# Routed experts between attention steps: the first product for 512 tokens at once instead of twice 256

## The chip, the cores and the metric

The kernel runs on one core of one Trainium2 chip. The metric is the device time of one execution in microseconds (us). PE is the matrix engine, PEld its weight loads, DVE the vector engine, ACT the scalar engine, POOL and SP the two engines that here mostly issue DMAs.

## The reference, cut to what matters

Two transformer layers run over 8 sequences of 512 tokens of 256 values, all in 32-bit floats. Layer 0 is a state-space block with a routed feed-forward part of 8 experts. Layer 1, which the change touches, adds two things to its input `x`: a 16-head attention and a top-2 routed feed-forward part with 7 experts and one "no-op" expert. Each expert takes at most 512 tokens (its capacity).

```python
# layer 1, attention: heads of 16 values, 512 x 512 scores for each of 8 sequences
scores = einsum('bhqd,bhkd->bhqk', qh, kh) * scale
scores = clip(clip(scores) * decay)          # a band that falls with |i - j|
out    = einsum('bhqk,bhkd->bhqd', softmax(scores), vh) @ Wo
# layer 1, experts: cap = 512 rows of 256 values for each of 7 experts, I = 1024
h   = relu(einsum('ceh,ehi->cei', inputs, experts_inter))     # first product
out = einsum('cei,eih->ceh', h, experts_out) * in_w[..., None]  # second product
combined = zeros.at[used_idx].add(out) + x_flat * (noop_w * noop_mask)[:, None]
```

## The kernel before, in words

The program writes the order of each engine's instructions by hand; an engine takes its own in that order and waits where data or a buffer is missing. Layer 0 fills the first two thirds of the span. Then comes the attention of layer 1, in 128 **steps** (the loop `for n in range(N + 2)`), one for each sequence `b`, group `g` of four heads, and block `c` of 128 keys. I count steps by `n`, from 0. In a step PE does two things for the attention:

- `scores` (L1554): four matmuls `s_ps` (L1561), each 16 rows of weights against 512 columns, into four PSUM banks of their own tag (`bufs=4`, so there is one set of banks). The four heads lie in four different row strips of the array and run side by side. DVE reads each bank once (L1564: times the band, maximum per row), which frees it. ACT then takes the exponent (L1578).
- `values` (L1584) of the step before the last: four matmuls `o_ps` (L1586), in four different column strips.

Between them PE is given other work by `fill()` (L1729). It has four places in a step: one after the scores, three after the values. Each call puts one **unit** there, from the first of these that has one: a piece already begun (`half_done`), an `urgent` piece (the output projection of a finished sequence, `finish`, L1517, matmuls `fin` at L1521), or the next unit of `experts()` (L1383), and this only while `spent < due()`. `spent` counts the expert units given so far, and `due()` (L1713) grows by the same amount each step, so that all `WORK` units are due at step `LAST` = 117. `WORK` is 238 before. The experts become ready at step 5, so `due()` grows by 238/110 = 2.16 units a step; the first unit goes out in step 8.

Before, an expert is worked in two halves of 256 rows. For each half the units are:

- **T**: four PE transposes (L1399) of the gathered rows into one bank, and a copy on ACT (L1400).
- **H**, eight of them: one block of 128 of the 1024 inner values. Two fp32 matmuls of 128 x 256 (L1407), which the profile shows as four instructions, and one ReLU on ACT (L1410).
- **Y**, eight of them: two fp32 matmuls of 128 x 256 (L1420), again four instructions. Four Y make the 256 outputs of 128 tokens; `yield True` after the first three marks the piece as begun, so the rest follow at the next places whatever `due()` says. After the fourth, ACT scales the result (L1426) and POOL adds it to `x1` in HBM by an indirect DMA (L1427).

I write **F** for a unit of `fin` (four such pieces in a row per sequence). T, H, Y and F share two PSUM banks of one tag (`bank`, L1363). The rows are gathered by indirect DMAs on POOL (`expert_rows`, L1367), two for each half, into two buffers; the two weight matrices of an expert, 1 MB each, come by SP's queue into one buffer each (`expert_w1`, L1378, and L1390).

A step's pattern is written as "after the scores | after the values": "H|H" has one unit in each place, "Y|YYY" one and three, "|" none. The order of PE's instructions can be read from the built program, so these patterns are known for both kernels.

Of the kernel before, what the change touches and what calls it, by code (L numbers as in the profile page):

```python
# [9 lines left out]
FP = mybir.dt.float32  # L10
I32 = mybir.dt.int32
AF = mybir.ActivationFunctionType
# [5 lines left out]
P = 128  # L18
B, S, DM = 8, 512, 256
NT = B * S  # L20
NTILE = NT // P
TPB = S // P
KC = DM // P
# [10 lines left out]
FC = FF // P  # L34
NBLK = (NT + NE * (P - 1)) // P
OFTEN = NBLK - 3
CAP = NT // NE
NE1 = NE - 1
NSLOT1 = NE1 * CAP
HALF = CAP // 2  # L40
# [23 lines left out]
def tile_kernel(ctx: ExitStack, tc: tile.TileContext, t, out: bass.AP):  # L64
    nc = tc.nc
    V, A, G, T, Y = nc.vector, nc.scalar, nc.gpsimd, nc.tensor, nc.sync
# [4 lines left out]
    def ctile(name, shape, dtype=FP, pool=None):  # L71
        return (pool or const).tile(shape, dtype, name=name, tag=name)
# [7 lines left out]
    ident = ctile("ident", [P, P])  # L80
# [38 lines left out]
    xn1 = dram.tile([NT + P, DM], FP, name="xn1", tag="xn1")  # L119
# [115 lines left out]
    def numbers(pool, table, to):  # L235

        none = pool.tile([P, table.shape[1]], FP, name="nu_n", tag="nu_n")
        V.tensor_scalar(none, table[:, :, 0], 0.0, nowhere, ALU.is_equal, ALU.mult)
        V.scalar_tensor_tensor(to, table[:, :, 0], -1.0, none, ALU.add, ALU.add)
# [134 lines left out]
    def bank(name, shape, tag="gen"):  # L374
        return mp.tile(shape, FP, name=name, tag=("e", "s")[tag] if isinstance(tag, int) else tag, bufs=2)
# [194 lines left out]
    with ExitStack() as es:  # L570
# [646 lines left out]
        e2 = None  # L1217
# [141 lines left out]
    with tc.tile_pool(name="a1", bufs=1) as p1, tc.tile_pool(name="a2", bufs=2) as p2, tc.tile_pool(  # L1359
        name="ap", bufs=1, space=PSUM  # L1360
# [3 lines left out]
            return psum.tile(shape, FP, name=name, tag="bank", bufs=2)  # L1364

        late_bank = bank
        def expert_rows(e, half):  # L1367
            xd = e2.tile([P, 2, DM], FP, name="e_xd", tag="e_rows")
            for c in range(2):
                at = e * TPB + half * 2 + c  # L1370
                G.indirect_dma_start(
                    out=xd[:, c, :], out_offset=None, in_=xn1,
                    in_offset=bass.IndirectOffsetOnAxis(ap=number1[:, at : at + 1], axis=0),
                    bounds_check=NT + P - 1, oob_is_err=True,
                )
            return xd

        def expert_w1(e):  # L1378
            w1 = e1.tile([P, KC, FF], FP, name="e_w1", tag="e_w1")
            Y.dma_start(out=w1, in_=t["ei"][e])  # L1380
            return w1

        def experts():  # L1383
            nonlocal number1
            number1 = e1.tile([P, NSLOT1 // P], I32, name="number1", tag="number1")
            numbers(e1, slots, number1)
            w1 = expert_w1(0)
            yield
            xd = expert_rows(0, 0)
            yield  # L1390
            for e in range(NE1):
                w2 = e1.tile([P, FC, DM], FP, name="e_w2", tag="e_w2")
                Y.dma_start(out=w2, in_=t["eo"][e])
                for half in range(2):
                    xdT = e1.tile([P, KC, HALF], FP, name="e_xdT", tag="e_xdT")
                    tp = bank("e_tp", [P, KC, HALF])
                    for k in range(KC):
                        for c in range(2):
                            T.transpose(tp[:, k, c * P : (c + 1) * P], xd[:, c, k * P : (k + 1) * P], ident)  # L1399
                    A.copy(xdT, tp)  # L1400

                    yield
                    hT = e1.tile([P, FC, HALF], FP, name="e_hT", tag="e_hT")
                    for f in range(FC):
                        hp = bank("e_hp", [P, HALF])
                        for k in range(KC):
                            T.matmul(  # L1407
                                hp, w1[:, k, f * P : (f + 1) * P], xdT[:, k, :], start=(k == 0), stop=(k == KC - 1)
                            )
                        A.activation(hT[:, f, :], hp, AF.Relu)  # L1410
                        yield
                    if half == 0:
                        xd = expert_rows(e, 1)
                    elif e + 1 < NE1:
                        w1, xd = expert_w1(e + 1), expert_rows(e + 1, 0)
                    yo = e2.tile([P, 2, DM], FP, name="e_yo", tag="e_yo")
                    for c in range(2):
                        yp = bank("e_yp", [P, DM])
                        for f in range(FC):
                            T.matmul(  # L1420
                                yp, hT[:, f, c * P : (c + 1) * P], w2[:, f, :], start=(f == 0), stop=(f == FC - 1)
                            )
                            if f % 2 == 1 and f < FC - 1:
                                yield True
                        at = e * TPB + half * 2 + c
                        A.mul(yo[:, c, :], yp, slots[:, at, 1:2])  # L1426
                        G.indirect_dma_start(  # L1427
                            out=x1, out_offset=bass.IndirectOffsetOnAxis(ap=number1[:, at : at + 1], axis=0),
                            in_=yo[:, c, :], in_offset=None, bounds_check=NT - 1, oob_is_err=False,
                            compute_op=ALU.add,  # L1430
                        )
                        yield
# [96 lines left out]
        def combine():  # L1529


            def add(b):
                G.dma_start(out=x_sb[:, b * TPB : (b + 1) * TPB, :], in_=rows_of(x1, b), accum_op=ALU.add)

            for b in (B - 1, *range(B - 2)):
                add(b)
            yield
            while B - 2 not in finished:
                yield
            add(B - 2)  # L1540
            for b in range(B - 1):
                G.dma_start(out=rows_of(out, b), in_=x_sb[:, b * TPB : (b + 1) * TPB, :])
# [149 lines left out]
        with tc.manual_schedule(engines=ENGINES):  # L1692
# [13 lines left out]
                G.memset(one, 0.0)  # L1706
            finished = set()
            urgent, idle, chains = [], [], []
            WORK = NE1 * 2 * (1 + FC + 2 * FC // 2)
            LAST = 117  # L1710
            spent = 0

            def due():  # L1713

                return WORK * (n - ready - 2) / (LAST - ready - 2)

            rows, work, ready, e1, number1 = combine(), None, None, None, None
# [28 lines left out]
            def more():  # L1746
                if spent == WORK:
                    next(rows, None)

            def follow():  # L1750

                nonlocal work, ready, e1, e2
                if late_left:
                    pass
                elif ready is None:
                    ready = n
                    tls.close()
                    e1 = es.enter_context(tc.tile_pool(name="f1", bufs=1, side="right"))
                    e2 = es.enter_context(tc.tile_pool(name="f2", bufs=2, side="right"))
                    work = experts()  # L1760
                    next(work)
                elif n == ready + 1:
                    next(work)
# [7 lines left out]
            for n in range(N + 2):  # L1771

                if n < N:
                    b, g, c = steps[n]
# [127 lines left out]
def build(arrays):  # L1902
    import concourse.bacc as bacc

    nc = bacc.Bacc("TRN2", target_bir_lowering=False, num_devices=1)
    t = {
        k: nc.dram_tensor(f"in_{k}_dram", v.shape, mybir.dt.from_np(v.dtype), kind="ExternalInput").ap()
        for k, v in arrays.items()
    }
    out = nc.dram_tensor("out_0_dram", (NT, DM), FP, kind="ExternalOutput").ap()  # L1910
    with tile.TileContext(nc) as tc:
        tile_kernel(tc, t, out)
    return nc
# [10 lines left out]
```

## Time and profile before

| | us |
|---|---|
| median of 3 runs (lowest, highest) | 1805.91 (1796.79, 1808.62) |
| the profiled execution, its own time | 1802.12 |
| its span, first to last instruction | 1800.4 |
| up to step 0 (layer 0) | 1137.2 |
| steps 0 to 7 | 70.5 |
| steps 8 to 118, with the expert units | 533.1 |
| step 119 to the end | 59.6 |

Over the span PE is busy 1630.7 us (91%), DVE 1201.4 (67%), ACT 914.8 (51%), POOL 574.7 (32%). The profile's page has the busy time of each engine, the span in 40 slices with the granted PE clock, the chain of work that ended last, and groups of equal instructions: first the busy time of the group, then the mean of one instruction in ns, then how long its engine had been idle before it and what ended that. A matmul counts as busy from its start to a modelled end, also while PE holds the next one back for a wait, so a PE that reads 100% can still stand. The chain and the timeline give start and length in us, then what ran, and how often.

### The profile page before, as it was taken

The page shows a single profiled execution, that of the slowest core. Times are in us where ns is not written, and L with a number is a line of the kernel's source. Part 1 is how long each engine was busy: PE and PEld are TensorE (multiplying, and loading weights), DVE is VectorE, ACT ScalarE, POOL GpSimd, SP SyncE. Part 2 cuts the span into 40 slices and gives each one's busy share as a digit, 9 for nine tenths or more (in the row PEclk, how much of TensorE's full clock was granted, in tenths as well). Part 3 has the DMA queues.
Part 4 walks back from the last instruction along what each step waited for, and adds up shares of the span by engine and source line. Part 5 has one row for each costly group of instructions (what it writes and reads, how often), then busy time and mean ns, then how long its engine had stood idle before and what let it go on. Part 6 is the DMA issues. An engine that isn't in the chain of part 4 may idle for free.

```text
span 1800.4 us, 25907 instructions
## 1 busy us (share of the span) xinstructions
PE 1630.7 (91%) x8736; PEld 980.5 (54%) x8736; DVE 1201.4 (67%) x3166; ACT 914.8 (51%) x2173; POOL 574.7 (32%) x520
## 2 busy tenths in 40 slices
PE   6556889989999999998798889879999999999997
PEld 6224567667677776775455556444544545444442
DVE  6578586575765765757877575566667666666674
ACT  4232344454454544544544523337767676766674
POOL 0041465475574654754323220001112111211030
PEclk8777799999999999999898898759999999999996
DMA  8010544554475445642644433232433324334163
GB/s 298 6 53 7 168 158 172 188 176 156 155 234 182 159 176 177 208 146 86 145 147 131 124 85 111 91 114 63 126 92 105 116 60 128 87 110 125 48 102 112
DMA packets 131789, 230.56 MB, mean 128 GB/s; under 512 B 20093, under 2 KB 93823, under 8 KB 120512
## 3 DMA queue, kind: packets, MB, share of 16 engines
q1 hardware_dynamic: 101952, 119.46, 21.4%
q0 software_dynamic: 28656, 108.69, 19.8%
q8 instruction: 73, 1.20, 0.3%
q10 hardware_dynamic: 1040, 0.66, 0.1%
q14 instruction: 68, 0.56, 0.1%
HBM read 176.23 MB, written 53.05 MB: 127 GB/s over the span
## 4 chain that ended last, share of the span: by engine, by line
PE 44%; DVE 6%; ACT 1%; issue 1%; DMA 0%; SPq 0%; POOL 0%; DVEq 0%; ACTq 0%
PE s_ps L1561 10%; PE o_ps L1586 8%; PE e_hp L1407 7%; PE e_yp L1420 6%; PE fin L1521 2%; PE qp L265 2%; PE pj L939 2%; PE tab L230 1%; PE pp L765 1%; DVE s L1564 1%; PE op L1084 1%; PE seg L1127 1%; PE yd L1165 1%; PE lp L250 1%; PE e_tp L1399 1%
## 5 line engine op out<-in xcount | busy, mean ns | idle before, releaser
L1564 DVE CUSTOM_DVE_ANT_0 s<-s_ps,band 128x512 f32<-128x512 f32 x512 | 322.9, 687 | 183.0 <-PE s_ps L1561 179.9
L1578 ACT ACTIVATE s<-s,ng 128x512 f32<-128x512 f32 x512 | 335.6, 711 | 0.0
L939 PE MATMUL pj<-xT,w_w_in 128*128 128x512 f32 x384 | 198.5, 643 | 11.7 <-DVE cv L952 7.5
L1561 PE MATMUL s_ps<-qT,kT 16*128 16x512 f32 x1024 | 198.7, 694 | 4.5 <-DMA kT<-kd 4.5
L1427 POOL DMA_INDIRECT x<-e_yo,number x28 | 44.7, 1597 | 445.7 <-ACT w L1574 291.0
L952 DVE SCALAR_TENSOR_TENSOR cv<-pj,w_conv_w,cv 128x511 f32<-128x511 f32 (+2 forms) x192 | 143.1, 746 | 20.5 <-ACT cv L948 16.0
L1111 POOL TENSOR_TENSOR au<-da,half 128x512 f32<-128x512 f32 x64 | 77.6, 1213 | 245.1 <-PE seg L1127 174.2
L1586 PE MATMUL o_ps<-s,wv 128*32 128x512 f32 x1024 | 154.5, 677 | 0.9 <-ACT w L1574 0.9
L642 PEld LDWEIGHTS h_ps<-xdT,w 128*128 128x128 f32 x1152 | 138.9, 194 | 21.3 <-issue 20.5
L642 PE MATMUL h_ps<-xdT,w 128*128 128x128 f32 x1152 | 142.1, 277 | 2.6 <-DMA w<-in_w_dram,w_idx 2.6
L666 PE MATMUL y_ps<-w,hT 128*128 128x256 f32 x576 | 137.9, 383 | 0.0
L1407 PEld LDWEIGHTS e_hp<-e_xdT,e_w 128*128 128x128 f32 x448 | 77.9, 191 | 87.3 <-issue 39.3
L666 PEld LDWEIGHTS y_ps<-w,hT 128*128 128x128 f32 x576 | 108.1, 193 | 29.8 <-issue 16.1
L1407 PE MATMUL e_hp<-e_xdT,e_w 128*128 128x256 f32 x448 | 124.2, 405 | 0.0
L939 PEld LDWEIGHTS pj<-xT,w_w_in 128*128 128x128 f32 x384 | 70.2, 201 | 92.8 <-issue 80.6
L1561 PEld LDWEIGHTS s_ps<-qT,kT 16*128 16x128 f32 x1024 | 66.5, 196 | 86.2 <-DVE peaks L1564 42.9
L1420 PE MATMUL e_yp<-e_w,e_hT 128*128 128x256 f32 x448 | 112.6, 394 | 0.0
L1420 PEld LDWEIGHTS e_yp<-e_w,e_hT 128*128 128x128 f32 x448 | 81.0, 191 | 54.1 <-issue 37.6
L1140 ACT ACTIVATE mt<-seg,mid 64x64 f32<-64x64 f32 x512 | 109.7, 309 | 0.8
L1174 DVE TENSOR_TENSOR yT<-yT,yd 128x512 f32<-128x512 f32 (+1 forms) x64 | 43.7, 683 | 98.0 <-PE yd L1165 97.0
L956 ACT ACTIVATE th<-cv 128x512 f32<-128x512 f32 x64 | 40.3, 630 | 120.1 <-DVE cv L952 107.4
L1159 DVE TENSOR_TENSOR mt<-mt,cbm 128x1024 f32<-128x1024 f32 x64 | 96.5, 1508 | 0.1
(340 smaller groups left out, 2819.8 us busy)
## 6 DMA issues: line engine op xcount, KB each, us to landing
ex<-exd SPq DMA_DIRECT2D x96, 128.0 KB
fr<-fdd SPq DMA_DIRECT2D x64, 128.0 KB
od<-os SPq DMA_DIRECT2D x28, 256.0 KB
e_w<-in_ei_dram SPq DMA_DIRECT2D x7, 1024.0 KB
e_w<-in_eo_dram SPq DMA_DIRECT2D x7, 1024.0 KB
vd<-vt SPq DMA_DIRECT2D x16, 272.0 KB
vt<-vd SPq DMA_DIRECT2D x8, 544.0 KB
u<-in_u_dram SPq DMA_DIRECT2D x8, 512.0 KB
```

The costliest lines, as they stand in the source:

```text
L642: T.matmul(hp[:, i, :], w1[:, k * FF + f * P : k * FF + (f + 1) * P], xdT[:, k * P : (k + 1) * P], start=(k == 0), stop=(k == KC - 1),)
L666: T.matmul(yp, hT[f // 4][:, f % 4, :], w2[:, f * DM : (f + 1) * DM], start=(f == 0), stop=(f == FC - 1),)
L939: T.matmul(pj, w_in[:, k, o * P : (o + 1) * P], self.xT[:, k, :], start=(k == 0), stop=(k == KC - 1))
L952: V.scalar_tensor_tensor(cv[:, s:], pj[:, : S - s], conv_w[:, q, 3 - s : 4 - s], cv[:, s:], ALU.mult, ALU.add)
L1140: A.activation(mt[lo, over, h], seg[lo, over, h], AF.Exp, bias=mid[lo, self.i, h : h + 1])
L1159: V.tensor_tensor(self.mt, self.mt, bc(self.cbm, 1, H3), ALU.mult)
L1407: T.matmul(hp, w1[:, k, f * P : (f + 1) * P], xdT[:, k, :], start=(k == 0), stop=(k == KC - 1))
L1420: T.matmul(yp, hT[:, f, c * P : (c + 1) * P], w2[:, f, :], start=(f == 0), stop=(f == FC - 1))
L1561: T.matmul(sp[i], self.k[r, cols], self.q[r, :], start=True, stop=True)
L1564: V.tensor_tensor_reduce(out=self.p[i], in0=sp[i], in1=band[:, at : at + S], scale=1.0, scalar=KEEP, op0=ALU.mult, op1=ALU.max, accum_out= ...
L1578: A.activation(self.p[i], self.p[i], AF.Exp, bias=self.ng[:, i : i + 1])
L1586: T.matmul(op[32 * i : 32 * i + 32, :], self.wv[:, i, :], self.p[i], start=(self.c == 0), stop=(self.c == TPB - 1),)
```

## The change

The first product is made for all 512 rows of an expert at once. The gathers of both halves are issued together (four instead of two). The transposes go by the two blocks of 128 input values: T is still four transposes into a bank of 128 x 512 and one copy, two T to an expert. H becomes two matmuls of 128 x 512 and one ReLU of 512 columns; eight H to an expert instead of sixteen. The second product keeps its shape and its sixteen Y. The next expert's first weights and gathers are asked for after the last H of an expert, ahead of its sixteen Y. `WORK` becomes 7 x (2 + 8 + 16) = 182; `LAST` and `due()` stay as they are.

```diff
-        def expert_rows(e, half):
-            xd = e2.tile([P, 2, DM], FP, name="e_xd", tag="e_rows")
-            for c in range(2):
...
+        def expert_rows(e):
+            halves = []
+            for half in range(2):
+                xd = e2.tile([P, 2, DM], FP, name="e_xd", tag="e_rows")
+                for c in range(2):
+                    at = e * TPB + half * 2 + c
+                    G.indirect_dma_start(
+                        out=xd[:, c, :], out_offset=None, in_=xn1,
...
+                halves.append(xd)
+            return halves
...
-            xd = expert_rows(0, 0)
+            halves = expert_rows(0)
             yield
             for e in range(NE1):
                 w2 = e1.tile([P, FC, DM], FP, name="e_w2", tag="e_w2")
                 Y.dma_start(out=w2, in_=t["eo"][e])
+                xdT = e1.tile([P, KC, CAP], FP, name="e_xdT", tag="e_xdT")
+                for k in range(KC):
+                    tp = bank("e_tp", [P, CAP])
+                    for c in range(TPB):
+                        T.transpose(
+                            tp[:, c * P : (c + 1) * P], halves[c // 2][:, c % 2, k * P : (k + 1) * P], ident
+                        )
+                    A.copy(xdT[:, k, :], tp)
+                    yield
+                hT = e1.tile([P, FC, CAP], FP, name="e_hT", tag="e_hT")
+                for f in range(FC):
+                    hp = bank("e_hp", [P, CAP])
+                    for k in range(KC):
+                        T.matmul(hp, w1[:, k, f * P : (f + 1) * P], xdT[:, k, :], start=(k == 0), stop=(k == KC - 1))
+                    A.activation(hT[:, f, :], hp, AF.Relu)
+                    yield
+                if e + 1 < NE1:
+                    w1, halves = expert_w1(e + 1), expert_rows(e + 1)
                 for half in range(2):
-                    xdT = e1.tile([P, KC, HALF], FP, name="e_xdT", tag="e_xdT")
-                    tp = bank("e_tp", [P, KC, HALF])
...
-                        hp = bank("e_hp", [P, HALF])
...
-                    if half == 0:
-                        xd = expert_rows(e, 1)
-                    elif e + 1 < NE1:
-                        w1, xd = expert_w1(e + 1), expert_rows(e + 1, 0)
                     yo = e2.tile([P, 2, DM], FP, name="e_yo", tag="e_yo")
                     for c in range(2):
+                        at = half * 2 + c
                         yp = bank("e_yp", [P, DM])
                         for f in range(FC):
                             T.matmul(
-                                yp, hT[:, f, c * P : (c + 1) * P], w2[:, f, :], start=(f == 0), stop=(f == FC - 1)
+                                yp, hT[:, f, at * P : (at + 1) * P], w2[:, f, :], start=(f == 0), stop=(f == FC - 1)
                             )
...
-            WORK = NE1 * 2 * (1 + FC + 2 * FC // 2)
+            WORK = NE1 * (KC + FC + 4 * FC // 2)
```

More of the change, by code (lines that the diff above doesn't have):

```diff
@@ L1366, in tile_kernel @@
         late_bank = bank
-        def expert_rows(e, half):
-            xd = e2.tile([P, 2, DM], FP, name="e_xd", tag="e_rows")
-            for c in range(2):
[L1370 to L1376, printed above, removed]
+        def expert_rows(e):
[6 more added lines that the diff above has]
+                        out=xd[:, c, :], out_offset=None, in_=xn1,
+                        in_offset=bass.IndirectOffsetOnAxis(ap=number1[:, at : at + 1], axis=0),
+                        bounds_check=NT + P - 1, oob_is_err=True,
+                    )
+                halves.append(xd)
+            return halves
         def expert_w1(e):
@@ L1393, in experts @@
                 Y.dma_start(out=w2, in_=t["eo"][e])
-                for half in range(2):
-                    xdT = e1.tile([P, KC, HALF], FP, name="e_xdT", tag="e_xdT")
-                    tp = bank("e_tp", [P, KC, HALF])
[L1397 to L1404, printed above, removed]
-                        hp = bank("e_hp", [P, HALF])
[L1406 to L1411, printed above, removed]
-                    if half == 0:
-                        xd = expert_rows(e, 1)
-                    elif e + 1 < NE1:
-                        w1, xd = expert_w1(e + 1), expert_rows(e + 1, 0)
+                xdT = e1.tile([P, KC, CAP], FP, name="e_xdT", tag="e_xdT")
[4 more added lines that the diff above has]
+                            tp[:, c * P : (c + 1) * P], halves[c // 2][:, c % 2, k * P : (k + 1) * P], ident
+                        )
+                    A.copy(xdT[:, k, :], tp)
[9 more added lines that the diff above has]
+                    w1, halves = expert_w1(e + 1), expert_rows(e + 1)
+                for half in range(2):
                     yo = e2.tile([P, 2, DM], FP, name="e_yo", tag="e_yo")
                     for c in range(2):
+                        at = half * 2 + c
                         yp = bank("e_yp", [P, DM])
@@ L1424, in experts @@
                                 yield True
-                        at = e * TPB + half * 2 + c
+                        at += e * TPB
                         A.mul(yo[:, c, :], yp, slots[:, at, 1:2])
```

## The prediction

> **What bounds the kernel now.** The page first. PE is the busiest engine, and its clock is not always full (first digit: slice 1 of 40):
>
> ```profile
> PE   6556889989999999998798889879999999999997
> ...
> PEclk8777799999999999999898898759999999999996
> ```
>
> I cut the span where the expert units begin and end (step 8, step 119) and asked for busy times in stretches; columns: stretch, length, then PE, PEld, DVE, ACT, POOL busy, the granted clock, DMA:
>
> ```profile
> 1207.69:1740.79 533.10, 533.10 (x2845) 255.85 (x2841) 348.30 (x1296) 366.93 (x764) 78.25 (x59) 0.97 0.34 95
> ```
>
> PE reads 100% there, DVE 65%, ACT 69%: PE is the bound, or stands with a matmul held back. The chain of waits in a short window tells (start, us, what, instructions):
>
> ```profile
> 1486.70 1.06 PE e_yp L1420 x4
> 1487.76 0.99 PE o_ps L1586 x8
> 1488.75 2.79 PE e_yp L1420 x12
> 1491.54 1.07 PE s_ps L1561 x8
> 1492.61 1.00 PE o_ps L1586 x8
> 1493.61 2.73 PE s_ps L1561 x7
> ...
> 1509.75 1.93 PE e_hp L1407 x8
> ```
>
> Read the Y first: 4 instructions take 1.06, 12 take 2.79, so one unit more in the same place costs 0.86, and a place costs 0.2 once. H is the same (8 take 1.93). An instruction of 256 columns is 0.215 us with no fixed part that shows, so half as many of 512 columns stream as long. Then s_ps: 1.07 usually, but 2.73 at 1493.61, after a step that had no unit at all. These 1.66 us are a hold, not work: the fourth score matmul needs the bank that DVE has not yet read (four reads, 2.44 us, begin only when the scores before are done).
>
> Third, the same place without any units, past the end of the experts (timeline: start, us, engine, line):
>
> ```profile
> 1740.79 1.14 PE L1561 MATMUL s_ps<-qT,kT 16*128 16x512 f32 x8
> 1741.86 1.06 PE L1586 MATMUL o_ps<-s,wv 128*32 128x512 f32 x8
> 1742.85 2.80 PE L1561 MATMUL s_ps<-qT,kT 16*128 16x512 f32 x8
> 1745.58 1.07 PE L1586 MATMUL o_ps<-s,wv 128*32 128x512 f32 x8
> 1746.58 1.92 PE L1561 MATMUL s_ps<-qT,kT 16*128 16x512 f32 x8
> ```
>
> A first light step leads to a hold of 1.66, a second in a row to one of 0.78 (1.85 to the next start, less 1.07): DVE then sets the pace, 2.86 a step.
>
> Fourth, the clock, in windows from the start of a step without units to the end of the step after it, and of one step near the end:
>
> ```profile
> 1491.47:1501.11 9.64, 9.64 (x49) 4.67 (x48) 6.42 (x23) 6.26 (x12) 1.63 (x1) 1.00 0.74 232
> 1501.11:1507.03 5.92, 5.92 (x34) 3.35 (x33) 3.78 (x13) 3.79 (x9) 3.81 (x3) 1.00 0.80 284
> ...
> 1652.04:1661.26 9.22, 9.22 (x37) 4.83 (x33) 6.29 (x23) 5.15 (x11) 2.83 (x3) 0.81 0.98 317
> 1762.69:1766.99 4.30, 4.30 (x19) 0.91 (x18) 3.00 (x13) 3.99 (x8) 0.00 (x0) 0.50 1.03 385
> ```
>
> A full step F|FFF is 5.92. No units and then Y|YYY is 9.64, so a single light step costs 9.64 - 5.91 = **3.73**, though it holds 2.07 of PE work. The third row is F|FFF alone, after a light step: 7.57 (9.64 - 2.07) would be usual, it took 9.22, at a mean clock of 0.81. The trace has the clock in windows of 3.41 us; one of them was granted half, for 1.65 us (1.58 to 1.65 at the other places where it can be compared; I use 1.61). Between steps 9 and 118 this happens seven times, each just after one of the 15 steps without units; nowhere else. [...]
>
> **The change, part by part.** *PE's own work.* H: 448 instructions of 256 columns become 224 of 512; the streaming stays. T: as many transposes. What goes is the 0.2 of places: summing all units of steps 8 to 118 in both built orders by the prices above gives 489.3 before, 480.5 after: **-8.8** if nothing held PE.
>
> *Pace.* WORK falls from 238 to 182, so units come at 182/110 = 1.65 a step, not 2.16, but H is twice as long. A piece of four Y runs through once begun, then waits for `due()`: 4/2.16 = 1.85 steps apart before, 4/1.65 = 2.42 after. The second product thus spreads over steps that have nothing beside it, and the doubled first product crowds into the others. In the built orders, steps by pattern (before, after, price):
>
> - none: 15, **34**, 3.73 (2.86 after another light one)
> - H|H: 34, 19; 4.19 before (1511.61 to 1515.79), 5.91 after (four old H, as Y|YYY)
> - Y|YYY: 22, 25; F|FFF 7, 7; 5.91
> - H alone: 0, 11; 2.07 + 1.92 = 3.99, just above the light floor
> - H|YYY: 6, 3; 5.91 before, 6.77 after. H|HH: 7, 0; 5.05
> - Y alone: 6, 3; T alone 4, 2; T|T 0, 3: floor 3.73
> - T with H: 10 (3.72 to 5.44), 4 (4.58 to 5.11)
>
> Sum before 519.4 (two light steps follow another). Measured 533.1; the seven half windows (7 x 1.61 = 11.3) and step 8, which starts at half clock (6.65 for T|HH, usual 4.58), fill the gap to 0.3. Sum after 532.2, with 11 light steps that follow a light one: **+12.8**.
>
> *Clock.* The 34 steps lie in 18 single and 8 double gaps. Singles at 7/15 and 1.61: 13.5. No double lies in the busy part of before: from nothing (the 60% streaming of a steady light step held the clock at steps 119 and 120) to both windows half, 3.2; I take one, 1.61, nearest to the single's price: 12.8. Together 26.3 less 11.3: **+15.0**. Ends: no window more than the seven, 0; every single one and doubles two, 18 x 1.61 + 8 x 3.2 - 11.3 = +43.
>
> [...]
>
> *ACT.* 112 ReLUs of 376 ns become 56; the nearest row, 512 columns from PSUM, is 597 (L267): 42.1 to 33.4 us. ACT is 69% busy, PE does not wait for it: 0. If a ReLU came late, H would wait for one of two banks; even now H and Y follow it with no hold in the chain.
>
> *Gathers, weights.* POOL issues four gathers in a row (1.14 each) where two stood, and the scatters queue behind them: 2.3 us on an engine 15% busy in the stretch. In before all four of the first expert were already issued by 1206.5. The next w1 and rows get sixteen Y of lead instead of eight; no wait of PE for either is in the trace. w2 still waits for the last Y and has two T and eight H (6 steps) to land: 0.
>
> *DVE.* In double gaps DVE sets the pace, so its side work counts (L1687, 0.68, or a wait for `sm`, at most 1.4): 0 to 5; I take 0, and 5 goes into the range.
>
> Sum: 1802.1 + 12.8 + 15.0 = **1829.9** for the profiled execution, which lies 3.8 under the median. Its half windows fall by chance, so I go half way: **1832**.
>
> **Rivals.** (1) *The clock holds in the new gaps.* Single light steps kept it 8 times of 15, and steady ones are 60% streaming. Against: seven drops. 1802 + 12.8 = 1815: within 1%. (2) *The places decide* (the other side). If the hold of a light step cost nothing, because what was put off leaves the later steps shorter, 8.8 would be saved: 1793, and 1782 if the seven half windows went too. It decides if DVE frees four banks within 1 us of the scores' end. Against: 2.44 of reads, a hold of 1.66 after each such step. (3) *The clock falls in every gap and stays down*, as in steps 124 to 126 (4.3 us each at 0.50): 1802 + 12.8 + 43 = 1858. For: with scores and values alone the clock does not rise. Against: every drop among units lasted one window. That the change doesn't do what it says is excluded by the built order.
>
> **Chances.** Forecast 0.80; (1) 0.13; (2) 0.03; (3) 0.04. About 1% is what a measurement of this kernel can tell from no change (1788 to 1824). Slower 0.82 (forecast less its low edge, and 3), same 0.16, faster 0.02. Range 1812 to 1850: down to (1), up to most of the unknown in doubles and DVE.
>
> **What would show it.** e_hp as 224 instructions of 512 columns, near 0.43 us apart; 34 steps without units, 3.73 or 2.86 each; some 17 to 20 half-clock windows between steps 9 and 118, for seven; the stretch of steps 8 to 118 near 561 for 533; all outside it equal. Wrong if holds after light steps are shorter, if the clock stays at 1.0, or if H after is held for a bank.

## The result, and the profile after

The changed kernel takes 1820.06 us (median of 8 runs, 1817.66 to 1827.25), the kernel before 1802.11 (8 runs, 1791.76 to 1815.06). The ratio is 1.0134, with a 95% interval of 1.0101 to 1.0166. It is slower, as forecast, and 1820 lies in the range given (1812 to 1850), 12 us under the point.

The profiled execution of after has a span of 1819.0 us. By stretches, with the mean of four profiles of each kernel (the later ones are told of below):

| us | before, first profile | after, first profile | before, mean of 4 | after, mean of 4 |
|---|---|---|---|---|
| layer 0, up to step 0 | 1137.2 | 1124.7 | 1132.7 | 1130.0 |
| steps 0 to 7 | 70.5 | 70.6 | 70.1 | 70.2 |
| **steps 8 to 118** | **533.1** | **564.2** | **532.4** | **559.7** |
| step 119 to the end | 59.6 | 59.6 | 58.4 | 60.6 |
| span | 1800.4 | 1819.0 | 1793.6 | 1820.4 |

The stretch with the expert units grew by 31.1 us in the first pair of profiles and by 27.3 on the mean. In the first pair, layer 0, which the change does not touch, happened to be 12.5 us shorter and hid part of it.

The clock row of the page, after:

```profile
PEclk8777999999999999999898988669989998999986
```

Slices 27 to 39 are the expert steps. The dips among the 9s are more than they were. The first line below is the whole stretch; then come, in the order of the lines, a gap of one step without units at full clock, with the Y|YYY behind it; the same of two such steps; and the same of two such steps with half-clock windows (stretch, length, then PE, PEld, DVE, ACT, POOL busy, the granted clock, DMA):

```profile
1195.23:1759.38 564.15, 562.25 (x2620) 232.29 (x2617) 347.25 (x1296) 362.19 (x708) 78.43 (x59) 0.94 0.32 91
1421.49:1431.13 9.64, 9.64 (x49) 4.67 (x48) 6.11 (x24) 5.67 (x11) 1.56 (x1) 1.00 0.31 70
1485.70:1498.19 12.49, 12.49 (x65) 5.61 (x64) 8.63 (x33) 8.80 (x17) 1.56 (x1) 1.00 0.23 55
1338.45:1355.13 16.68, 16.68 (x66) 6.99 (x65) 9.62 (x36) 8.92 (x17) 1.55 (x1) 0.69 0.26 72
```

The single gap costs 9.64 - 5.91 = 3.73, just as before. The double one costs 12.49 - 5.91 = 6.58 (forecast 3.73 + 2.86 = 6.59). The last took 4.19 more, with three half-clock windows in it. PE reads busy all the time in all three; the chain of waits in the last shows what that hides (start, us, what, instructions):

```profile
1338.52 1.07 PE s_ps L1562 x8
1339.59 1.00 PE o_ps L1587 x8
1340.59 2.76 PE s_ps L1562 x7
1343.35 1.87 PE o_ps L1587 x8
1345.21 2.33 PE s_ps L1562 x8
1347.54 2.00 PE e_yp L1421 x4
1349.54 1.87 PE o_ps L1587 x8
1351.41 3.79 PE e_yp L1421 x12
1355.20 1.07 PE s_ps L1562 x8
```

The first hold is the 2.76. Then the clock is half: values take 1.87 in place of 1.00, one Y 2.00 in place of 1.06, until it comes back within the three Y at 1351. The groups by line in the stretch, after (busy, mean ns of one, idle before):

```profile
L1562 PE MATMUL s_ps<-qT,kT 16*128 16x512 f32 x888 | 183.2, 667 | 0.0
L1410 PE MATMUL e_hp<-e_xdT,e_w 128*128 128x512 f32 x224 | 112.8, 627 | 0.0
L1411 ACT ACTIVATE e_hT<-e_hp 128x512 f32<-128x512 f32 x56 | 33.0, 590 | 54.1 <-PE e_hp L1410 53.4 <-issue 0.7
```

The first product itself became shorter, 124.2 to 112.8 us. The score matmuls, of which there are as many as before, went from 159.9 to 183.2: that is the holds, put down to the instruction that is held, and the half clock.

### The profile page after: what moved, and what is told of

It is laid out like the page before. It is cut to its first block, busy times and chain, and to the rows that moved or that the text cites. A ratio compares the mean times of both kernels' runs of the same rounds, so it can differ in the third digit from the quotient of the medians.

```text
span 1819.0 us, 25441 instructions
## 1 busy us (share of the span) xinstructions
PE 1650.5 (91%) x8512; PEld 951.2 (52%) x8512; DVE 1195.9 (66%) x3166; ACT 910.1 (50%) x2117; POOL 572.7 (31%) x520
## 4 chain that ended last, share of the span: by engine, by line
PE 43%; DVE 7%; ACT 1%; issue 1%; DMA 1%; POOL 0%; ACTq 0%; DVEq 0%; POOLq 0%
PE s_ps L1562 11%; PE o_ps L1587 8%; PE e_yp L1421 6%; PE e_hp L1410 6%; PE fin L1522 2%; PE qp L265 1%; PE tab L230 1%; PE pj L939 1%; PE op L1084 1%; PE pp L765 1%; DVE s L1565 1%; DVE mt L1159 1%; PE e_tp L1401 0%; PE seg L1127 0%; DVE yT L1010 0%
## 5 line engine op out<-in xcount | busy, mean ns | idle before, releaser
L1562 PE MATMUL s_ps<-qT,kT 16*128 16x512 f32 x1024 | 222.6, 714 | 4.6 <-DMA kT<-kd 4.6
L1587 PE MATMUL o_ps<-s,wv 128*32 128x512 f32 x1024 | 160.4, 699 | 0.9 <-ACT w L1575 0.9
L1562 PEld LDWEIGHTS s_ps<-qT,kT 16*128 16x128 f32 x1024 | 77.6, 201 | 119.5 <-DVE peaks L1565 71.7
L1421 PE MATMUL e_yp<-e_w,e_hT 128*128 128x256 f32 x448 | 119.6, 412 | 0.0
L1421 PEld LDWEIGHTS e_yp<-e_w,e_hT 128*128 128x128 f32 x448 | 85.1, 201 | 62.4 <-issue 50.1
L1410 PE MATMUL e_hp<-e_xdT,e_w 128*128 128x512 f32 x224 | 112.8, 627 | 0.0
L948 ACT ACTIVATE cv<-pj,w_conv_b,w_conv_w 128x512 f32<-128x512 f32 x64 | 49.8, 778 | 86.6 <-PE pj L939 81.2
L1159 DVE TENSOR_TENSOR mt<-mt,cbm 128x1024 f32<-128x1024 f32 x64 | 91.5, 1430 | 0.7 <-ACT mt L1140 0.5
```

The source lines that it names most:

```text
L1159: V.tensor_tensor(self.mt, self.mt, bc(self.cbm, 1, H3), ALU.mult)
L1410: T.matmul(hp, w1[:, k, f * P : (f + 1) * P], xdT[:, k, :], start=(k == 0), stop=(k == KC - 1))
L1421: T.matmul(yp, hT[:, f, at * P : (at + 1) * P], w2[:, f, :], start=(f == 0), stop=(f == FC - 1))
L1562: T.matmul(sp[i], self.k[r, cols], self.q[r, :], start=True, stop=True)
L1587: T.matmul(op[32 * i : 32 * i + 32, :], self.wv[:, i, :], self.p[i], start=(self.c == 0), stop=(self.c == TPB - 1),)
```

## The experiments

Theory A: the loss comes from the pace, by steps without a unit and by the half clock that follows them. Theory B: it comes from the wide product, or from the gathers, turns and weights that moved with it. All changes are to the kernels named; of each run I give steps 8 to 118 ("the stretch") and the number of half-clock windows that begin in steps 10 to 118, from its profile. Windows in steps 8 and 9 belong to the start, at which the clock is still half (0.57 on the mean of the two steps in the first profile of after); I speak of them by themselves.

### The loss without the wide product

Before, with two H to a unit:

```diff
                         A.activation(hT[:, f, :], hp, AF.Relu)
-                        yield
+                        if f % 2 == 1:
+                            yield
...
-            WORK = NE1 * 2 * (1 + FC + 2 * FC // 2)
+            WORK = NE1 * 2 * (1 + FC // 2 + 2 * FC // 2)
```

> The kernel before, with its 256-column first product and its two halves, but two H given as one unit (WORK 182). In the built order 33 steps have no unit, as against 15 before and 34 after. Theory A (the pace makes the loss: steps without units, and the half clock after them): steps 8 to 118 take 555 to 566 us, with 12 to 22 half-clock windows, and the whole is 20 to 33 us slower than before. Theory B (the wide product itself, or the gathers and weights moved with it, make the loss): the stretch stays near 533, the whole within 5 us of before.

Measured: the stretch takes 550.5 us with 9 half windows; the whole 1815.84 (4 runs), ratio to before 1.0115 (1.0052 to 1.0178).

```profile
1205.38:1755.83 550.45, 549.84 (x2845) 272.34 (x2841) 347.12 (x1296) 369.96 (x764) 82.17 (x59) 0.97 0.34 93
```

The matmuls are those of before (2845 on PE in both stretches). Most of the loss is there, 18 us of the 27 in the stretch: fewer, larger units do that much without the wide matmul. Both numbers lie below what A expected: only 9 windows were half (16 in the first profile of after). The full-clock sum of its order is 530.7, near the 532.2 of after; 9 x 1.6 and the start make up most of the rest.

### The new order with narrow units

After, with each H in two units of 256 columns:

```diff
-                    hp = bank("e_hp", [P, CAP])
-                    for k in range(KC):
...
+                    for half in range(2):
+                        r = slice(half * HALF, (half + 1) * HALF)
+                        hp = bank("e_hp", [P, HALF])
+                        for k in range(KC):
+                            T.matmul(hp, w1[:, k, f * P : (f + 1) * P], xdT[:, k, r], start=(k == 0), stop=(k == KC - 1))
+                        A.activation(hT[:, f, r], hp, AF.Relu)
+                        yield
...
-            WORK = NE1 * (KC + FC + 4 * FC // 2)
+            WORK = NE1 * (KC + 2 * FC + 4 * FC // 2)
```

> The kernel after (all rows gathered and turned, all of the first product ahead of all of the second), but each H made as two units of 256 columns (WORK 238). 17 steps have no unit. Theory A: steps 8 to 118 take 533 to 542 us with 6 to 11 half-clock windows, the whole within 9 us of before. Theory B, if the moved gathers, weights and turns are at fault: near 560, 20 us or more slower.

Measured: 540.0 us with 7 half windows; the whole 1807.74 (10 runs), ratio 1.0068 (1.0021 to 1.0116).

```profile
1195.60:1735.64 540.04, 537.32 (x2844) 256.66 (x2841) 348.13 (x1296) 366.49 (x764) 75.01 (x59) 0.97 0.34 94
```

All that moved with the change is still there, gathers, turns, weights, the first product ahead of the second, and 20 of the 27 us are gone. Most of the loss is not theirs. Of the 8 us that are left over before, about 3 lie in step 8: it took 9.39 where its work sums to 4.25 (5.1 over), against 2.1 to 2.4 over in the four profiles of before. These 3 do go with the moved gathers (see the start, below).

### The wide product with the old pace

After, with an H counted as two:

```diff
                     A.activation(hT[:, f, :], hp, AF.Relu)
-                    yield
+                    yield "wide"
...
-                        spent += queue[0] is work
-                        if next(queue[0]):
+                        got = next(queue[0])
+                        spent += (queue[0] is work) * (2 if got == "wide" else 1)
+                        if got is True:
...
-            WORK = NE1 * (KC + FC + 4 * FC // 2)
+            WORK = NE1 * (KC + 2 * FC + 4 * FC // 2)
```

> The kernel after, with the wide H, but an H counts as two units in the pace (WORK 238). 21 steps have no unit, all of them single ones. Prices of the prediction: 517 for the stretch at full clock, 2 to 8 for the start at half clock, 21 x 7/15 x 1.6 = 16 for half windows. Theory A: 533 to 541 us, the whole within 8 us of before. Theory B (the wide product at fault): the stretch stays near 564.

Measured: 546.2 us with 11 half windows; the whole 1807.85 (4 runs), ratio 1.0101 (1.0028 to 1.0174).

```profile
1198.55:1744.79 546.24, 543.30 (x2621) 224.65 (x2617) 347.52 (x1296) 362.35 (x708) 73.48 (x58) 0.96 0.32 92
```

The direction is A's, the size is 5 us over its range. What was missed: once in most sequences DVE waits for a DMA. It fetches `sm`, the softmax sums that were written to HBM some steps before, and in the table of waits (who waited for whom: us in all, times, the longest) the stretch has:

```profile
DVE low L1681 <- DMA sm<-od: 11.4, 5, 2.6
```

A step with a wide H alone has only 3.99 us of PE work, and DVE's 2.86 leaves little slack in it for such a wait: the steps behind it (13, 29, 61 and 77, among others) took 5.1 to 7.0. With one more wait that is put down to another DMA, `low` stood 14.3 us for DMAs here, and 2.1 in the first profile of after.

### The clock alone

After, with work for PE in the steps that got no unit:

```diff
+                if ready is not None and ready + 3 <= n <= LAST and not given[0]:
+                    T.matmul(bank("warm", [P, DM]), ident, band[:, :DM], start=True, stop=True)
+                    T.matmul(bank("warm", [P, DM]), ident, band[:, :DM], start=True, stop=True)
                 follow()
```

(`given[0]` counts the units of the step.)

> The kernel after, with two extra fp32 matmuls of 128 x 256 on constant data, written to a bank that nobody reads, at the end of each of the 34 steps that got no unit (1.06 us of PE each, inside the hold of 1.66). Theory A: the holds stay (532 + 3 for the stretch at full clock, 8 for the start), but the half-clock windows after step 10 go from 16 to at most 3: 541 to 548 us in place of 564, the whole 16 to 23 us faster than the kernel after. If the clock is not what costs the second half of the loss, the stretch stays at 560 to 570 or grows by 34 x 1.06.

Measured: 543.0 us, **no** half window; the whole 1813.19 (10 runs), ratio to before 1.0054 (1.0010 to 1.0098). The stretch, then its first gap, in the chain of waits, and as one stretch with the Y|YYY behind it:

```profile
1209.43:1752.44 543.01, 541.39 (x2756) 230.67 (x2753) 348.81 (x1296) 362.02 (x708) 76.67 (x59) 0.99 0.34 94
```

```profile
1252.26 1.07 PE s_ps L1562 x8
1253.33 1.00 PE o_ps L1587 x8
1254.32 0.63 PE warm L1830 x2
1254.95 0.43 PE warm L1831 x2
1255.38 1.67 PE s_ps L1562 x8
1257.05 1.06 PE e_yp L1421 x4
```

```profile
1252.19:1261.83 9.64, 9.64 (x54) 4.77 (x53) 5.81 (x22) 5.67 (x11) 1.62 (x1) 1.00 0.12 14
```

The extra matmuls take 1.06, the hold after them shrinks from 1.66 to 0.60 (1.67 less 1.07), and the gap takes the same 9.64. So the hold is DVE's time: it ends no later with 1.06 us of PE work in it, and with this work no window from step 10 on was half. This separates the two parts of the loss. The stretch loses 17 us (against the mean of after) to 21 (against the first profile), which is what half clock cost there. It is still 10.6 us over the mean of before, but that one has half windows of its own, 6.5 at 1.6, some 10 us. Against before without them it is about 21 over: 5 from a slower start, and 16 from the holds and the added matmuls (of these, 3 were expected). The whole improved by less than the 16 to 23 us expected: by 7 in the medians, by 13 to 14 if the ratios to before are compared. The one profile has 1139.1 us of layer 0, 9 more than the mean of after.

### No steps without a unit

Two kernels in which the Y of a piece are paced one by one. The first is the one with the wide H counted as two, the second the kernel before:

```diff
-                while queue := half_done or urgent or (idle if idle and spent < due() else []):
+                while queue := (
+                    (half_done if urgent or spent < due() else []) if half_done
+                    else urgent or (idle if idle and spent < due() else [])
+                ):
```

> The kernel after, with a wide H counted as two units (WORK 238) and with the four Y of a piece paced one by one: a begun piece goes on only when the pace asks for it or when a projection is due. No step is left without a unit, 3 are light. Prices of the prediction: 490 for the stretch at full clock, 2 to 8 for the start, 0 to 3 half-clock windows. Theory A: steps 8 to 118 take 493 to 508 us, the whole 20 to 40 us faster than before and 40 to 60 faster than after. Theory B, that a bank held by a piece over several steps makes PE wait for ACT or DVE instead: 525 or more.

> The kernel before (256 columns, two halves) with the four Y of a piece paced one by one. No step without a unit, none light; 497 at full clock, 2 to 5 for the start. Theory A: steps 8 to 118 take 498 to 508 us, the whole 20 to 35 us faster than before, and the wide product is worth at most 7 us once the holds are gone (spread against this one). Theory B: 525 or more.

Measured: the wide one 507.5 us with 1 half window, 1766.62 in all (6 runs), ratio to before 0.9832 (0.9788 to 0.9877). The narrow one 506.6 with none, 1766.69 (6 runs), ratio 0.9808 (0.9759 to 0.9858). The stretches, wide and narrow:

```profile
1200.54:1708.01 507.47, 502.85 (x2621) 198.86 (x2617) 349.93 (x1296) 361.80 (x708) 69.72 (x53) 0.99 0.34 98
1215.00:1721.62 506.62, 500.51 (x2845) 233.31 (x2841) 350.34 (x1296) 365.52 (x764) 71.98 (x53) 1.00 0.35 99
```

Both are faster than both kernels: than before by 30 and 35 us, by their ratios, and than after by 53 in the medians. The chain of waits in the wide one, in the second product:

```profile
1318.45 1.07 PE s_ps L1562 x8
1319.52 1.06 PE e_yp L1421 x4
1320.58 1.00 PE o_ps L1587 x8
1321.57 1.06 PE e_yp L1421 x4
1322.63 1.07 PE s_ps L1562 x8
```

One Y in each of two places, 4.19 a step, no score matmul held here. The score matmuls of the wide one's stretch now sum to 137.3 us:

```profile
L1562 PE MATMUL s_ps<-qT,kT 16*128 16x512 f32 x889 | 137.3, 644 | 0.0
```

Two things were not as expected. The wide H, worth 7 us by its saved places, is worth nothing (507.5 against 506.6). And the narrow kernel, with an expected 498 to 508, is at the upper end. In both, T and H can now follow each other in one place, and PE waits for ACT's copies; the timeline of such a step of the wide one (start, us, engine, line, and in brackets the idle time before it):

```profile
1493.66 1.09 PE L1401 MATMUL e_tp<-ident,e_xd 128*128 128x128 f32 x8
...
1494.99 1.13 PE L1410 MATMUL e_hp<-e_xdT,e_w 128*128 128x512 f32 x2 [0.24 <-ACT e_xdT L1404]
...
1496.69 1.12 PE L1410 MATMUL e_hp<-e_xdT,e_w 128*128 128x512 f32 x2 [0.58 <-ACT e_xdT L1404]
```

That step took 7.22 where its work sums to 5.97. But such waits do not eat up the 7 us, for the narrow kernel has more of them. From the tables of waits of the two stretches, wide (first two lines) and narrow:

```profile
PE e_hp L1410 <- ACT e_xdT L1404: 1.6, 4, 0.6
DVE low L1681 <- DMA sm<-od: 12.0, 6, 2.7
PE e_hp L1407 <- ACT e_xdT L1400: 5.3, 6, 1.7
DVE low L1680 <- DMA sm<-od: 4.0, 5, 1.3
```

(One more wait of `low` in each, 2.7 and 2.3, is put down to another DMA.) What the wide one has beyond the narrow one is a slower start (10.31 for 5.11, against 6.62 for 4.58: 3 us) and DVE's waits for `sm`. Beside or just behind these, six steps with a wide H alone took 4.2 to 5.3 in place of 3.98, 5 us in sum, and step 13, with the one half window, took 6.92. That the DMA ends too late because these steps are short is my reading; no run varied it.

### Is layer 0 shorter, or was it chance

Both kernels again, unchanged:

> The kernel after, unchanged, once more. In its first profile layer 0, whose code and order are those of before, took 1124.7 us where before took 1137.2. If that is chance (where half-clock windows fall in the last 250 us of layer 0), it lies between 1120 and 1142 here, steps 8 to 118 take 558 to 570, and the whole is 18 to 34 us slower than before. If the changed kernel makes layer 0 shorter, it is 1122 to 1128 again.

> The kernel before, unchanged, for a second profile. If layer 0 varies by chance it differs from 1137.2 by several us; steps 8 to 118 take 530 to 538 with 5 to 10 half-clock windows.

> The kernel before, a third profile. Open is why the whole moved by 18 to 24 us when steps 8 to 118 moved by 28 to 31. If that is chance in layer 0, layer 0 lies anywhere in 1120 to 1145 here and steps 8 to 118 take 530 to 536.

> The kernel after, a third profile. If chance: layer 0 in 1120 to 1145, not below that of before on the mean of the profiles by more than 4 us; steps 8 to 118 take 556 to 566, with 13 to 18 half-clock windows. If the change really shortens layer 0: below 1128 here and on the mean.

> The kernel before, a fourth profile, for the mean: layer 0 in 1120 to 1145 by chance, steps 8 to 118 in 530 to 536.

> The kernel after, a fourth profile, for the mean: layer 0 in 1120 to 1145 if it varies by chance, below 1128 if the change shortens it; steps 8 to 118 in 556 to 566.

Measured, layer 0 / the stretch / half windows:

| profile | before | after |
|---|---|---|
| 1 | 1137.2 / 533.1 / 7 | 1124.7 / 564.2 / 16 |
| 2 | 1127.2 / 530.0 / 5 | 1135.1 / 557.8 / 14 |
| 3 | 1141.0 / 533.1 / 7 | 1132.2 / 557.7 / 14 |
| 4 | 1125.5 / 533.4 / 7 | 1128.0 / 559.1 / 15 |

The second time, after took 1820.73 (6 runs) and its ratio was 1.0128 (1.0079 to 1.0177). Layer 0 varies by 15.5 us within before and by 10.4 within after, and the two means differ by 2.7: chance is enough, and nothing here shows that the change shortens it. The stretches do not overlap. From one profile of each, the difference of the wholes could have been read as 18.6 us with a gain of 12.5 in layer 0 that the other profiles do not bear out.

## Why the prediction was right, and by how much it was off

**PE's own work: right.** An instruction of 512 columns costs here what two of 256 do: those of H mostly start 0.429 us apart in after, 0.216 in before. The places saved show in the group of H (124.2 to 112.8 us), and PE's gain reached nobody, since DVE set the pace of the light steps (the single gap takes 9.64 in both kernels).

**Pace and light steps: right in kind and size.** 34 steps without units, 3.73 for a single gap and 6.58 for the double one shown (forecast 3.73 and 6.59; the four double gaps at full clock took 6.58 to 7.0). The kernel with no half window checks the sum at full clock, forecast as 532.2 after and 519.4 before: its 543.0 less 7.4 for its slow start is 535.6. The mean of before, less 10.5 for its half windows and 2.2 for its start, is 519.7. That is 15.9 more where 12.8 was forecast, and 3 were expected for the added matmuls. What makes the hold is a little wider than the prediction put it: not the fourth score matmul alone waits for DVE, each of the four goes when its own bank is read. In before, behind the light step at 1491.47, they start at 1493.54, 1494.00, 1494.61 and 1495.22, and DVE's four reads end at 1493.32, 1493.93, 1494.54 and 1495.15.

**Clock: right in kind, the term too large.** Forecast +15.0 from 16.3 windows at 1.61; the 7/15 in it is a count, and what decides whether a gap brings a half window no run isolates. In the first profile there were 16: 7 in 6 of the 18 single gaps (8.4 forecast), 9 in 4 of the 8 double gaps (8 forecast). Priced step by step against the same gap at full clock, the 7 cost 11.3 us, but the 9 only 11.5: each 1.3. I read it so that part of a half window inside a double gap falls into time in which PE would have been held anyway; no run tests that. 22.8 less the 11.3 of before is +11.5. On the mean of four there were 14.75 windows for 6.5.

**Gathers: wrong, 0 was forecast.** The step of the prediction said that all four gathers of the first expert were issued in time. They were issued, but the first T now needs all four landed, where before it needed two. PE's timeline in step 8, after:

```profile
1197.25 0.69 PE L1401 MATMUL e_tp<-ident,e_xd 128*128 128x128 f32 x2
1199.01 0.48 PE L1401 MATMUL e_tp<-ident,e_xd 128*128 128x128 f32 x1 [1.07 <-DMA e_xd<-xn,number]
1200.31 0.48 PE L1401 MATMUL e_tp<-ident,e_xd 128*128 128x128 f32 x1 [0.83 <-DVE wv L1583]
1200.72 1.94 PE L1587 MATMUL o_ps<-s,wv 128*32 128x512 f32 x8
1202.59 1.12 PE L1401 MATMUL e_tp<-ident,e_xd 128*128 128x128 f32 x4
```

Two idle times of 1.07 and 0.83 stand between the transposes (the second is put down to DVE, but the weight load of the same transpose waits 1.12 for the gather), and the step holds no H. Two to three half windows begin in step 8 of after, one in step 8 of before. Steps 8 and 9 cost 4.4 to 7.7 us over their full-clock price in the four profiles of after, step 8 of before 2.1 to 2.4 over its own. I had carried the 2.1 over. This term was +3.2 on the mean.

**ACT and weights: right.** ReLUs 41.9 to 33.0 us (forecast 42.1 to 33.4), no hold of PE for them in after; none for w1 or w2.

**DVE's side work:** 0 taken, up to 5 allowed; what remains of the first profile's 31.1 when the terms above are taken off (12.8, 11.5, and 5.6 for its start) is some 1 us.

**The sum.** For the stretch 27.8 was forecast and 27.3 is the mean of four; part of the closeness is that too much for the clock and nothing for the start cancel. That the whole came out at 1820, not 1832, lies outside the working of the stretch. The profiled execution of before, 1802.1, on which the sum was built, was a long one (the mean span of four profiles is 1793.6, not 1800.4), and I moved the sum up by 2 for the median besides. That is not all of it: the medians of before are 1802.1 and, in later rounds, 1799.5 and 1799.7, so by the medians the whole grew by 18 and 21 us in the two rounds, by the ratios 24 and 23, and by the mean spans 27. How far the scatter of layer 0 makes up these differences is not shown.

**Rivals.** The clock held in none of the four profiles of after, so rival 1 is out; the kernel with added matmuls shows the stretch when the clock does hold, 543. Rival 2, that the places decide, fails on its own condition: DVE's four reads take 2.44, not under 1 us, and the gap takes the same 9.64 when PE has work in the hold. Rival 3 fails too: 10 of the 26 gaps of the first profile had a half window (6 single, 4 double), and none had more than three.

## What to carry to other kernels

Where filler work is paced by a count of units, a change that alters the size of a unit alters the pace: re-weigh the count by time, and see which steps get nothing. Here a step that got nothing cost 3.73 us by the loop of the other engine, and in 10 of the 26 gaps of the first profile half clock besides; one unit in each place brought the stretch of the kernel before from 533 to 507 us, where the saved starts of the wide product had been put at 8.8. Before reading a difference of 1% from one profile of each kernel, find a stretch that the change cannot touch and see how much that stretch varies.

## What the hardware showed beyond that

- **The half clock came without a pause of PE.** The trace has the granted clock in pieces of 3.41 us or a multiple of it. In the first profile of before, I summed for each window of 3.41 us between steps 9 and 118 the time that PE streamed (0.429 us for 512 columns of an instruction, the distance at which those of H start in after, and each of the four strip matmuls of scores or values as a quarter, for the four start within 0.02 us of each other where nothing holds them). The seven windows followed by a half one have 1.65 us or less, the 140 others at full clock 1.71 or more; in the first profile of after the ten followed by a half one have 1.66 or less, the 135 others 1.70 or more. In the other profiles the border lies at 1.64 to 1.73, where both happen. One window does not fit: in the narrow kernel with paced Y the one from 1431.03 has 1.33, with PE idle for 1.73 of it, and the clock stayed full. If instead all time counts in which anything streams, nothing is sorted: in a hold the heads start one behind the other, 0.46 to 0.61 us apart, and the seven windows of before have 2.86 to 3.05 us, others at full clock as little as 2.76. So PE reads busy in a hold, and it does work, but with one or two heads at a time in place of four. The sum is a description, not the rule: what the clock counts, no run here isolates.
- **Scores and values alone did not bring it back.** In steps 124 to 126 of before (with one transposition of 0.48 beside them) PE reads 100% busy at 0.50, 4.3 us a step, for the whole time; among the expert units of before and after each drop lasted one or two windows of 3.41 us behind a single gap, two or three at a double one (first profiles).
- **Layer 0, which is the same in all these kernels, varied from 1124.7 to 1144.6 us** over the fourteen profiles, and the time it spent at half clock from 147 to 184 us in the eight of before and after. By and large the two go together (147 us: 1124.7 and 1128.0; 181 and 184 us: 1141.0, 1137.2 and 1132.2). What sets that from one execution to the next was not tried.
